# An earlier weight load, row-tiled products and a square root by Newton steps in a convolution network on one core

## The chip, the core and the metric

The kernel runs on one core of a Trainium2 chip. Its time is the device time of one execution in microseconds (us), the median over several executions of the same program. The engines are TensorE (PE, with PEld for its weight loads), VectorE (DVE), ScalarE (ACT), GpSimd (POOL) and SyncE (SP), which issues most DMAs. Every engine takes its own instructions strictly in the order in which the program was written; they meet through semaphores.

## The reference

The input x has shape 4 x 32 x 32 x 16 (batch, height, width, channels). Four layers each add to it a function of its group norm:

```python
x = x + conv(gn(x), M0, W0, G0)
x = x + conv(gn(x), M1, W1, G1)
x = x + interval(gn(x), W0, b0, W1, b1, W2, b2)
x = x + conv(gn(x), M3, W3, G3)
```

`gn` takes 8 groups of 2 channels: for each batch and group it subtracts the mean over the image and both channels, and divides by the root of the variance plus 1e-5. `conv` is the costly part:

```python
kern = transpose(G, (0, 1, 5, 4, 2, 3)).reshape(h * w * f, c, 3, 3)
shifted = conv_general_dilated(x, kern, 'SAME')   # 1024 x 16 output planes of 1024
diff = relu(x - shifted)                          # for each i, j and each y, x
return einsum('ijyx,byxc->bijc', M, x) - einsum('ijyx,bijyxc->bijc', W, diff)
```

For each of 1024 positions ij and 16 filters there is a 3x3 convolution of the whole image, a relu, and a sum weighted by W. The product with M is called the first terms below.

`interval` takes the 32 x 32 image as a table over intervals (i, j). It forms running maxima and minima over all subintervals (`interval_pooling`), and then two steps of the form `g = sigmoid(f[i,k] @ Wf + r[k,j] @ Wr + b)`, `max over k`, and a last sigmoid of a product.

## The kernel before

**Tiling.** The two batches 2g and 2g+1 are one group g, with 2 x 16 = 32 channels (`GC`). There are three convolutions (layers 0, 1, 2 in the code) and two groups, hence 6 phases in the order (g0, layer 0), (g1, layer 0), (g0, layer 1) and so on; the interval layer lies between layers 1 and 2. A phase has 8 chunks of 128 output positions ij, which are the 128 rows of PSUM. A chunk has 32 steps, one for each filter f and batch b. There are 1536 steps. A unit is 4 filters, so 8 steps, and there are 192 units; the first two ("plain") are prepared in another way.

**A step.** It uses one pair of PSUM banks, `pc` (two banks of 128x512, since the image has 1024 points). Numbers are split into a high and a low part[...]; `ia`, `ib`, `iyz` and `im9` are arrangements of the shifted image, and `WU`, `WL`, `WD`, `W9` are the split weights of a unit (the first three are the tile `parts`). Each product has 64 rows; two of them, on the upper and lower halves of the array (row tiles 0 and 1), run side by side. `first_part` issues 8 products (L627) from `parts` with `ib` and `ia`, and ACT multiplies the pair by 1 + EPS (L663). `second_part` of the step before then adds 6 products with `iyz` and `im9`, and one DVE instruction (L680, output `junk`) takes min(sum, 0) times the W chunk `WT` and accumulates it to one column. The pool has four bank pairs, which rotate.

**Units.** The generator `prep_parts` prepares a unit's weights during the eight steps of another unit, one `yield` a step. Slot 1: DVE splits the high part off (L203). Slot 2: ACT writes W9 (L175). Slot 3: ACT writes WD (L236), POOL writes WL (L237) and adds to W9 (L238). Slot 4: ACT WU (L240), POOL four more (L241, L243, L245). Slot 5: `prep(u + 1)`, POOL's subtraction of the identity from the next unit's raw weights (L214). Slot 7: SP issues two DMAs that copy `parts` across partitions (L251), then `load_raw(u + RAWS)` (L110), 768 KB from HBM into one of two `raw` buffers; L203 of that unit waits for its L214. A unit is ready one to two units before its first use.

**Work beside the steps.** `behind(phase)` is a generator that prepares the next phase: norms, interval layer, the image's new arrangement, first terms. What it yields is the number of steps to go on before its next piece, or IDLE, or CALM; with these two it waits for a slot of the unit which says so. So it is interleaved at fixed places into every engine's order:

```python
may = next(parts, (IDLE, CALM)) if n or at >= FIRST else (IDLE, CALM)
...
wait -= 1
if wait <= 0 and (kind > 0 or kind in may):
    kind = wait = next(behind, 1 << 20)
```

`group_norm` sums on DVE (L316 to L337), forms the mean, `xc` and its square on POOL (L344 to L348), sums the squares, and takes the root of the variance on ACT (L358) and its inverse on DVE (L360), after which POOL writes the normalized image (L361) to `xn` or, for the interval layer, to `xi`. The root and the interval layer's sigmoid need different tables of ACT; a small activation of `spare` (L353) ahead of the root brings the table load before the value is there. After it, `before_conv` transposes (L375, DVE), writes to DRAM and back (`xs<-xt` L381, `raw<-xs` L392, SP), splits (`upper_x` L203, L280, L284), and places the parts (L298, L300 on SP, `iyz` L288 on POOL, L175 and L178). `interval_layer` transposes `xi` (L508, DVE), scans, and takes products: the right side in three pieces of 11 columns k (`right_side` L561, copied by ACT L564) and the left side (L548), then sums (POOL, L580), maxima (DVE, L587) and a sigmoid (L594), whose table is loaded by another activation of `spare` (L591).

Of the kernel before, what the change touches and what calls it, by code (L numbers as in the profile page):

```python
# [8 lines left out]
F32 = mybir.dt.float32  # L9
F32R = mybir.dt.float32r  # L10
I32 = mybir.dt.int32
AF = mybir.ActivationFunctionType
# [3 lines left out]
P = 128  # L16
# [28 lines left out]
def net_kernel(ctx: ExitStack, tc: tile.TileContext, x, xq, xi, convs, iv_w, iv_b, out):  # L45
# [174 lines left out]
    def prep_parts():  # L220

        for u in range(PLAIN, n_chunks * NU):
            parts = wpool.tile([P, 2, 3, FU, P], F32R, tag="parts", bufs=AHEAD + 1, name=f"parts_{u}")
            W9 = wpool.tile([P, FU, P], F32R, tag="W9", bufs=AHEAD + 1, name=f"W9_{u}")
            units[u] = [parts[:, :, k] for k in range(3)] + [W9]
            src = raws.pop(u)
            w8 = src[:, 0].rearrange("p f k -> p (f k)")  # L230
            WU, WL, WD = (parts[:, 0, k].rearrange("p f k -> p (f k)") for k in range(3))
            high = upper(src[:, 0:1], 1, f"w{u}")[:, 0]
            yield (IDLE,)
            halve(W9, src[:, 1], low_w)
            yield ()
            nc.scalar.activation(WD, high, AF.Copy, scale=-EPS)  # L236
            nc.gpsimd.tensor_tensor(WL, w8, high, ALU.subtract)  # L237
            nc.gpsimd.tensor_tensor(W9, W9.bitcast(F32), src[:, 2], ALU.add)  # L238
            yield ()
            nc.scalar.copy(WU, high)  # L240
            nc.gpsimd.tensor_tensor(WD, WD.bitcast(F32), WL.bitcast(F32), ALU.add)  # L241
            for lo, hi in QUARTERS:
                nc.gpsimd.tensor_copy(WU[hi], WL[lo].bitcast(F32))  # L243
            for lo, hi in QUARTERS:
                nc.gpsimd.tensor_copy(WL[lo], high[hi])  # L245
            yield ()
            prep(u + 1)
            yield (IDLE,)
            yield (IDLE, CALM)
            for h in range(2):  # L250
                nc.sync.dma_start(  # L251
                    parts[64 * h : 64 * h + 64, 1].bitcast(F32),
                    parts[64 - 64 * h : 128 - 64 * h, 0].bitcast(F32),
                )
            load_raw(u + RAWS)
            yield (IDLE, CALM)
            yield (IDLE, CALM)

# [50 lines left out]
    def pair_view(ap):  # L309
        return ap.rearrange("p t (g s) -> p t g s", s=2)  # L310

    def group_norm(g, name, dst, gap):


        def sums(src):
            nc.vector.tensor_reduce(  # L316
                part[:, : GC // 2], src.rearrange("p t (g s) -> p g t s", s=2), axis=AX.XY, op=ALU.add
            )

        def totals(name):  # L320
# [26 lines left out]
        sq = work.tile([P, NT, GC], F32, tag="sq", name=f"sq_{name}")  # L347
        nc.gpsimd.tensor_tensor(sq, xc, xc, ALU.mult)  # L348
        yield 4
        sums(sq)  # L350
        yield gap
        yield IDLE
        nc.scalar.activation(spare, spare, AF.Sqrt)  # L353
        v = yield from totals(f"v{name}")
        yield 2
        yield IDLE
        rstd = work.tile([P, GC // 2], F32, tag="rstd", name=f"rstd_{name}")
        nc.scalar.activation(rstd, v, AF.Sqrt, bias=eps, scale=1.0 / (2 * NP))  # L358
        yield 2
        nc.vector.reciprocal(rstd, rstd)  # L360
        nc.gpsimd.tensor_tensor(pair_view(dst), pair_view(xc), spread(rstd), ALU.mult)  # L361
        yield 3

# [54 lines left out]
    def first_terms(layer, mt):  # L418


        sums = bank_pair(f"pf_{layer}")
        for g in range(NG):
            for pt in range(NT):
                for j in range(4):
                    nc.tensor.matmul(  # L425
                        sums[32 * j : 32 * j + 32, g, :256],
                        lhsT=xns[g][:, pt, :], rhs=mt[:, pt, j, :],
                        start=pt == 0, stop=pt == NT - 1, tile_position=(0, 32 * j),
                    )
        ft = work.tile([P, NG, NT * GC], F32, tag="fs", name=f"ft_{layer}")  # L430
        for g in range(NG):
            nc.vector.transpose(ft[:, g], sums[:, g, : NT * GC])
        yield 1
        for g in range(NG):
            nc.vector.tensor_tensor(
                X[g], X[g], ft[:, g].rearrange("p (t m) -> p t m", t=NT), ALU.add
            )
            yield 1
# [7 lines left out]
    def constants():  # L446
        nc.sync.dma_start(wv, iv_w)
        nc.sync.dma_start(bv, iv_b)
        mask2 = const.tile([P, GB], F32, name="mask2")
        nc.vector.tensor_reduce(  # L450
            mask2, ident.rearrange("p (s b c) -> p b s c", b=GB, c=C), axis=AX.XY, op=ALU.add
        )

        nc.gpsimd.tensor_scalar_mul(mask2[GC : 2 * GC], mask2[GC : 2 * GC], -1.0)
        yield 2

        def blocks(dst, k, mask, n, p0=0):
            p = dst.shape[0]
            nc.gpsimd.tensor_tensor(
                dst,  # L460
                wv[p0 : p0 + p, k, :].unsqueeze(1).to_broadcast([p, n, C]),
                mask[p0 : p0 + p].unsqueeze(2).to_broadcast([p, n, C]),
                ALU.mult,
            )

        nc.gpsimd.memset(rt, 0.0)
        yield 1


        for k, hidden, name in ((0, None, "f0"), (3, 2, "f1"), (6, 5, "f2")):  # L470
            n = 64 if hidden is None else 96
            t = const.tile([n, GB, C], F32, name=name)
            blocks(t[:64], k, mask2, GB)
            if hidden is not None:
                blocks(t[64:], hidden, mask2, GB, 64)
            iv[name] = t.rearrange("p k c -> p (k c)")
            yield 1
        for k, name in ((1, "r0"), (4, "r1")):
            t = const.tile([64, NQ * GB, C], F32, name=name)
            for q in range(NQ):  # L480
                blocks(t[:, q * GB : (q + 1) * GB, :], k, mask2, GB)
            iv[name] = t.rearrange("p k c -> p (k c)")
            yield 1
    def interval_layer(g):
# [37 lines left out]
        def running(dst, src):  # L522
# [16 lines left out]
            out=r[:R, :H, 1:], in_=table(one), pattern=[[-1, H], [1, H]], compare_op=ALU.is_ge,  # L539
            fill=0.0, base=0, channel_multiplier=0,  # L540
        )
        yield 5

        def left(name, wf):
# [9 lines left out]

        def right_side(name, wr):

            for k0 in range(0, T1, 11):
                j0 = k0 + 1
                ps = bank(f"ps_{name}{g}{k0}")
                n = T1 - j0  # L560
                nc.tensor.matmul(  # L561
                    ps[:, : 11 * n], lhsT=wr, rhs=r[:R, k0 : k0 + 11, j0:], start=True, stop=True
                )
                nc.scalar.copy(  # L564
                    rt[:, j0:, k0 : k0 + 11],
                    ps[:, : 11 * n].rearrange("p (k j) -> p j k", j=n),
                )
                yield 1

        def step(name, ftp, bias):  # L570
# [17 lines left out]
                last = t  # L588
                yield 6 if i < QI else 3
            yield IDLE  # L590
            nc.scalar.activation(spare, spare, AF.Sigmoid)  # L591
            yield 2
            yield IDLE
            nc.scalar.activation(s, s, AF.Sigmoid, bias=bias)  # L594
# [385 lines left out]
```

## Time and profile before

| quantity | value |
|---|---|
| median of 3 runs | 2479.14 us |
| lowest and highest | 2478.43 and 2481.91 us |
| the profiled execution, its time | 2478.41 us |
| span of its trace | 2476.7 us |
| granted TensorE clock | 1.0 of full speed |
| busy: PE / PEld / DVE / ACT / POOL | 99 / 84 / 84 / 76 / 64 % of the span |
| L680 `junk`, 1536 times | 1224 ns each |
| L663, 1520 times | 1008 ns each |
| L627, 21504 matmuls in four groups | 379 to 388 ns each, two at a time |
| POOL of a unit: L237, L238, L241 / L243, L245 / L214 | 1308, 1303, 1299 / 608, 609 / 1052 ns |
| one raw load, issue to landing | 7.1 us |
| DMA, share of 16 engines | some 53 % |

A row of the profile names an operation by its line, engine and tile. The busy shares are averages over the span; what a change at one place is worth is read from the timeline around that place.

### The profile page before, as it was taken

To read this page: it belongs to the slowest core of one execution; us is meant where nothing else is said; L and a number is where in the kernel's file an instruction comes from. 1 tells how busy PE (TensorE), PEld (TensorE's weight loads), DVE (VectorE), ACT (ScalarE), POOL (GpSimd) and SP (SyncE) were. 2 spreads that over 40 slices of the span, in tenths; PEclk is the share of its full clock that TensorE was granted. 3 is DMA by queue.
4 is the path that set the end of the run, shared out by engine and by line. 5 is a ranking of instruction groups with operands and counts; after the bars stand their busy time and mean duration, and the time that the engine had idled before them with its cause. 6 is when DMAs were issued, how large, how long until landed. Compare 5 with 4: busy or idle time off the path is not lost.

```text
span 2476.7 us, 58058 instructions
## 1 busy us (share of the span) xinstructions
PE 2458.2 (99%) x21906; PEld 2090.1 (84%) x21906; DVE 2087.3 (84%) x3617; ACT 1878.4 (76%) x2181; POOL 1579.7 (64%) x1750
## 2 busy tenths in 40 slices
PE   8999999999999999999999999999999999999999
PEld 5999888888888888888888988888998888888887
DVE  9888878888888888778898988899889888788887
ACT  4778767787777778777777777787777787677776
POOL 4766655666565657555567777586878676555552
PEclk9999999999999999999999999999999999999999
DMA  6446754466454467644454545574455467554442
GB/s 198 138 137 182 203 155 135 124 182 164 133 143 135 135 168 198 186 116 134 136 145 127 142 124 140 146 196 125 126 138 144 127 181 195 154 148 137 137 137 54
DMA packets 97673, 366.92 MB, mean 148 GB/s; under 512 B 26480, under 2 KB 31472, under 8 KB 97392
## 3 DMA queue, kind: packets, MB, share of 16 engines
q1 hardware_dynamic: 96832, 362.79, 53.0%
q8 instruction: 172, 2.82, 0.5%
q14 instruction: 109, 0.89, 0.1%
q10 hardware_dynamic: 432, 0.39, 0.1%
q0 software_dynamic: 128, 0.02, 0.0%
HBM read 199.78 MB, written 1.02 MB: 81 GB/s over the span
## 4 chain that ended last, share of the span: by engine, by line
PE 94%; DVE 2%; issue 1%; DMA 1%; ACT 0%; SPq 0%; POOL 0%; ACTq 0%; DVEq 0%; POOLq 0%
PE pc L627 93%; DVE junk L680 1%; PE pf L425 1%; DMA raw<-in_g 1%; ACT pc L663 0%; DMA first<-in_g 0%; SPq L298 0%; DVE raw L846 0%; SPq L300 0%; PE ps_l L548 0%; PE ps_r L561 0%; DMA parts<-parts 0%; DVE tables L508 0%; DVE raw L854 0%; DMA ib<-first 0%
## 5 line engine op out<-in xcount | busy, mean ns | idle before, releaser
L680 DVE SCALAR_TENSOR_TENSOR junk<-pc,WT 128x1024 f32<-128x1024 f32 x1536 | 1879.5, 1224 | 359.1 <-PE pc L627 308.3
L663 ACT ACTIVATE pc<-pc 128x1024 f32<-128x1024 f32 x1520 | 1532.0, 1008 | 561.0 <-PE pc L627 535.8
L627 PE MATMUL pc<-ib,parts 64*128 64x512 f32 x6080 | 958.5, 388 | 4.1 <-DVE junk L680 3.4
L627 PE MATMUL pc<-iyz,parts 64*128 64x512 f32 x6080 | 955.5, 387 | 2.2 <-ACT pc L663 2.0
L627 PE MATMUL pc<-ia,parts 64*128 64x496 f32 x6080 | 933.5, 379 | 0.0
L627 PEld LDWEIGHTS pc<-ia,parts 64*128 64x128 f32 x6080 | 595.5, 184 | 100.8
L627 PEld LDWEIGHTS pc<-ib,parts 64*128 64x128 f32 x6080 | 591.5, 184 | 105.0 <-DVE junk L680 9.9
L627 PEld LDWEIGHTS pc<-iyz,parts 64*128 64x128 f32 x6080 | 592.5, 184 | 88.4 <-ACT pc L663 6.4
L627 PE MATMUL pc<-im,W 64*128 64x496 f32 x3072 | 611.5, 384 | 0.0
L237 POOL TENSOR_TENSOR parts<-raw,upper_w 128x512 fp32r<-128x512 f32 x190 | 248.5, 1308 | 500.2 <-DVE upper_w L203 434.8
L627 PEld LDWEIGHTS pc<-im,W 64*128 64x128 f32 x3072 | 303.0, 184 | 54.5 <-issue 3.2
L243 POOL CAST parts<-parts 32x512 fp32r<-32x512 f32 x380 | 231.1, 608 | 50.1 <-ACT parts L240 31.8
L238 POOL TENSOR_TENSOR W<-W,raw 128x512 fp32r<-128x512 f32 x190 | 247.6, 1303 | 1.8 <-ACT W L175 1.8
L241 POOL TENSOR_TENSOR parts<-parts 128x512 fp32r<-128x512 f32 x190 | 246.8, 1299 | 2.0 <-ACT parts L236 1.9
L245 POOL CAST parts<-upper_w 32x512 fp32r<-32x512 f32 x380 | 231.6, 609 | 22.8
L214 POOL TENSOR_TENSOR raw<-raw,ident 128x512 f32<-128x512 f32 x190 | 199.9, 1052 | 52.2 <-DMA raw<-in_g 28.7
L175 ACT ACTIVATE W<-raw,low_w 128x512 fp32r<-128x512 f32 x190 | 136.2, 717 | 0.1
L680 DVE DVE_READ_ACCUMULATOR junk<-pc,WT 128x1 f32 x1536 | 127.5, 83 | 0.0
L236 ACT ACTIVATE parts<-upper_w 128x512 fp32r<-128x512 f32 x190 | 118.8, 625 | 6.6 <-DVE upper_w L203 6.4
L240 ACT CAST parts<-upper_w 128x512 fp32r<-128x512 f32 x190 | 116.5, 613 | 0.0
L695 POOL TENSOR_SCALAR acc<-acc 128x32 f32<-128x32 f32 x40 | 16.4, 409 | 141.7 <-DVE junk L680 139.7
L203 DVE TENSOR_SCALAR upper_w<-raw 128x512 int32<-128x512 int32 x190 | 86.1, 453 | 1.2 <-POOL raw L214 0.9
(139 smaller groups left out, 479.4 us busy)
## 6 DMA issues: line engine op xcount, KB each, us to landing
raw<-in_g SPq DMA_DIRECT2D x190, 768.0 KB, 7.1
parts<-parts SPq DMA_DIRECT2D x380, 384.0 KB, 4.9
WT<-in_w SPq DMA_DIRECT2D x48, 512.0 KB, 4.6
MT<-in_mt SPq DMA_DIRECT2D x24, 512.0 KB, 7.4
raw<-xs SPq DMA_DIRECT2D x120, 71.8 KB, 2.9
ib<-temp SPq DMA_DIRECT2D x40, 128.0 KB, 2.6
ia<-temp SPq DMA_DIRECT2D x80, 62.0 KB, 3.4
ib<-first SPq DMA_DIRECT2D x8, 128.0 KB, 2.4
```

Source lines behind the costliest of these rows:

```text
L175: nc.scalar.activation(dst, src, AF.Copy, scale=mask[:, 1:2])
L214: eng.tensor_tensor(raws[u][:, s, at:to], raws[u][:, s, at:to], pick[s][:, f0 + at : f0 + to].unsqueeze(2).to_broadcast([P, to - at, P]), ...
L236: nc.scalar.activation(WD, high, AF.Copy, scale=-EPS)
L237: nc.gpsimd.tensor_tensor(WL, w8, high, ALU.subtract)
L238: nc.gpsimd.tensor_tensor(W9, W9.bitcast(F32), src[:, 2], ALU.add)
L240: nc.scalar.copy(WU, high)
L241: nc.gpsimd.tensor_tensor(WD, WD.bitcast(F32), WL.bitcast(F32), ALU.add)
L243: nc.gpsimd.tensor_copy(WU[hi], WL[lo].bitcast(F32))
L245: nc.gpsimd.tensor_copy(WL[lo], high[hi])
L627: nc.tensor.matmul(ps[:, h, at : at + n], lhsT=w[r], rhs=v[r] if n == NH else v[r][:, :n], start=first and k == 0, stop=k == len(pairs) - ...
L663: nc.scalar.activation(ps, ps, AF.Copy, scale=1.0 + EPS)
L680: nc.vector.scalar_tensor_tensor(junk, ps.rearrange("p h n -> p (h n)"), 0.0, chunks[n], op0=ALU.min, op1=ALU.mult, accum_out=accs[phase][ ...
```

## The change

Five edits.

1. In `prep_parts` the subtraction `prep(u + 1)` is written two slots earlier (behind L238 in slot 3, ahead of L241), and `load_raw(u + RAWS)` three slots earlier (at the end of slot 4).
2. `right_side` uses one bank pair. The piece of 352 columns runs on row tile 0 into bank 0, the pieces of 231 and 110 on row tile 1 into bank 1. For that the lower 64 partitions need a copy of r, `below` (POOL), and the constants r0 and r1 are made on 128 partitions.
3. `group_norm` takes the inverse root without ACT: POOL forms a = v / (2 NP) + 1e-5, DVE forms a first value y from a's bits with a shift and a subtraction, and POOL improves it in four rounds y = y (1.5 - 0.5 a y y) of four instructions each, with the pauses 1, 1, IDLE, 2 ahead of them.
4. With it go the root's activation of `spare` and, in the interval layer, the sigmoid's.
5. The sigmoid's activation of `spare` is issued once, behind the products of layer 0's first terms.

```diff
             nc.gpsimd.tensor_tensor(W9, W9.bitcast(F32), src[:, 2], ALU.add)
+            prep(u + 1)
             yield ()
             nc.scalar.copy(WU, high)
...
                 nc.gpsimd.tensor_copy(WL[lo], high[hi])
+            load_raw(u + RAWS)
             yield ()
-            prep(u + 1)
             yield (IDLE,)
             yield (IDLE, CALM)
             for h in range(2):
...
-            load_raw(u + RAWS)
             yield (IDLE, CALM)
             yield (IDLE, CALM)
...
+    def inverse_root(v, name):
+
+        n = GC // 2
+        a, y, t = (
+            work.tile([P, n], F32, tag=tag, name=f"{tag}_{name}") for tag in ("root_a", "root_y", "root_t")
+        )
+        nc.gpsimd.tensor_scalar(a, v, 1.0 / (2 * NP), 1e-5, op0=ALU.mult, op1=ALU.add)
+        nc.vector.tensor_scalar(
+            t.bitcast(I32), a.bitcast(I32), 1, None, op0=ALU.logical_shift_right
+        )
+        nc.vector.tensor_scalar(
+            y.bitcast(I32), t.bitcast(I32), -1.0, float(0x5F3759DF), op0=ALU.mult, op1=ALU.add
+        )
+        nc.gpsimd.tensor_scalar_mul(a, a, -0.5)
+        for pause in (1, 1, IDLE, 2):
+            yield pause
+            nc.gpsimd.tensor_tensor(t, a, y, ALU.mult)
+            nc.gpsimd.tensor_tensor(t, t, y, ALU.mult)
+            nc.gpsimd.tensor_scalar(t, t, 1.5, None, op0=ALU.add)
+            nc.gpsimd.tensor_tensor(y, y, t, ALU.mult)
+        return y
...
-        nc.scalar.activation(spare, spare, AF.Sqrt)
         v = yield from totals(f"v{name}")
-        yield 2
-        yield IDLE
-        rstd = work.tile([P, GC // 2], F32, tag="rstd", name=f"rstd_{name}")
-        nc.scalar.activation(rstd, v, AF.Sqrt, bias=eps, scale=1.0 / (2 * NP))
-        yield 2
-        nc.vector.reciprocal(rstd, rstd)
+        rstd = yield from inverse_root(v, name)
         nc.gpsimd.tensor_tensor(pair_view(dst), pair_view(xc), spread(rstd), ALU.mult)
...
+        if layer == 0:
+            nc.scalar.activation(spare, spare, AF.Sigmoid)
         ft = work.tile([P, NG, NT * GC], F32, tag="fs", name=f"ft_{layer}")
...
-        nc.gpsimd.tensor_scalar_mul(mask2[GC : 2 * GC], mask2[GC : 2 * GC], -1.0)
+        for at in (GC, 3 * GC):
+            nc.gpsimd.tensor_scalar_mul(mask2[at : at + GC], mask2[at : at + GC], -1.0)
...
-            t = const.tile([64, NQ * GB, C], F32, name=name)
+            t = const.tile([P, NQ * GB, C], F32, name=name)
...
+        below = tables[R:, : T1 * T1].rearrange("p (i j) -> p i j", j=T1)
+        nc.gpsimd.tensor_copy(below, r[:R])
+        tops = (r[:R], below)
         yield 5
...
-            for k0 in range(0, T1, 11):
+            ps = bank_pair(f"ps_{name}{g}")
+            blocks = []
+            for k0, h, at in ((0, 0, 0), (11, 1, 0), (22, 1, 11 * (T1 - 12))):
                 j0 = k0 + 1
-                ps = bank(f"ps_{name}{g}{k0}")
                 n = T1 - j0
+                blocks.append((k0, j0, n, ps[:, h, at : at + 11 * n]))
                 nc.tensor.matmul(
-                    ps[:, : 11 * n], lhsT=wr, rhs=r[:R, k0 : k0 + 11, j0:], start=True, stop=True
+                    blocks[-1][3], lhsT=wr[R * h : R * h + R], rhs=tops[h][:, k0 : k0 + 11, j0:],
+                    start=True, stop=True,
                 )
+            for k0, j0, n, sums in blocks:
                 nc.scalar.copy(
...
             yield IDLE
-            nc.scalar.activation(spare, spare, AF.Sigmoid)
             yield 2
```

More of the change, by code (lines that the diff above doesn't have):

```diff
@@ L555, in right_side @@
         def right_side(name, wr):
-            for k0 in range(0, T1, 11):
+            ps = bank_pair(f"ps_{name}{g}")
+            blocks = []
+            for k0, h, at in ((0, 0, 0), (11, 1, 0), (22, 1, 11 * (T1 - 12))):
                 j0 = k0 + 1
-                ps = bank(f"ps_{name}{g}{k0}")
                 n = T1 - j0
+                blocks.append((k0, j0, n, ps[:, h, at : at + 11 * n]))
                 nc.tensor.matmul(
-                    ps[:, : 11 * n], lhsT=wr, rhs=r[:R, k0 : k0 + 11, j0:], start=True, stop=True
+                    blocks[-1][3], lhsT=wr[R * h : R * h + R], rhs=tops[h][:, k0 : k0 + 11, j0:],
+                    start=True, stop=True,
                 )
+            for k0, j0, n, sums in blocks:
                 nc.scalar.copy(
-                    rt[:, j0:, k0 : k0 + 11],
-                    ps[:, : 11 * n].rearrange("p (k j) -> p j k", j=n),
+                    rt[:, j0:, k0 : k0 + 11], sums.rearrange("p (k j) -> p j k", j=n)
                 )
```

## The prediction

> **What bounds the kernel.** I read the page first (busy shares, the chain that ended last), then the waits, then timelines around the places where TensorE stops.
>
> ```profile
> PE 2458.2 (99%) x21906; PEld 2090.1 (84%) x21906; DVE 2087.3 (84%) x3617; ACT 1878.4 (76%) x2181; POOL 1579.7 (64%) x1750
> PE 94%; DVE 2%; issue 1%; DMA 1%; ACT 0%; SPq 0%; POOL 0%; ACTq 0%; DVEq 0%; POOLq 0%
> L237 POOL TENSOR_TENSOR parts<-raw,upper_w 128x512 fp32r<-128x512 f32 x190 | 248.5, 1308 | 500.2 <-DVE upper_w L203 434.8
> ```
>
> TensorE is the bound and idles 18.5 us of 2476.7, 12 of it before the first 50 us; POOL mostly waits. So the change can win only at the few stops left, and it can make new ones. In the PE timelines one step (14 products) starts every 1.57 us. Four bank pairs rotate, so the reduction L680 (`junk`) of step j must end before the first product of step j+4, which without a stop starts 3.81 us after the second part of j (1284.72 to 1288.53). One stop shows the rule, in the DVE and PE timelines:
>
> ```profile
> 1283.67 1.31 DVE L508 STREAM_TRANSPOSE tables<-xi 32x256 f32<-32x256 f32 x2
> 1286.28 1.30 DVE L508 STREAM_TRANSPOSE tables<-xi 32x256 f32<-32x256 f32 x2
> 1287.61 1.23 DVE L680 SCALAR_TENSOR_TENSOR junk<-pc,WT 128x1024 f32<-128x1024 f32 x1
> 1288.90 0.73 PE L627 MATMUL pc<-ib,parts 64*128 64x512 f32 x4 [0.21 <-DVE junk L680]
> ```
>
> The junk ends at 1288.84 with its accumulator, TensorE starts at 1288.90 instead of 1288.53: 0.37 lost, and about 0.11 more to refill (the next product pair is 0.33 apart instead of 0.22). DVE may thus be about 1.5 us late unpunished.
>
> **What the Trainium skill says.** "ScalarE: Activation LUTs", What ACT_TABLE_LOAD costs: 1283 ns per load, plus a drain; the ACT timeline agrees on 1283 ns. "Perfetto Trace Analysis", Tensor Engine Instruction: ACT, DVE and GpSimd run strictly in order, and ends of matmuls are estimates; so a late POOL result blocks the DVE instruction and every junk behind it. "DMA: Bandwidth & Descriptors", Queues, rings and completion order: on each DMA engine the descriptors of one queue are taken in ring order; the trace agrees: small loads issued behind `raw<-in_g` (1594.84) landed at 1604.1 to 1605.1, just after its 1603.94. "TensorEngine Tiling (Array Packing)", Gotcha 1: different row tiles write to different banks; the change puts its two halves in two banks.
>
> **Part 1, table loads.** The program's order on ACT has five loads before and two after: the one at the start, and one behind layer 0's first terms, where TensorE has 7.04 us of other products (L425), so it costs nothing. Four go, each a stop like this one:
>
> ```profile
> 1564.04 1.28 ACT L353 ACT_TABLE_LOAD   x1
> 1565.33 0.20 ACT L353 ACTIVATE spare<-spare 1x1 f32<-1x1 f32 x1
> 1565.44 1.00 ACT L663 ACTIVATE pc<-pc 128x1024 f32<-128x1024 f32 x1
> ```
>
> TensorE's product at 1566.49 came 0.55 late, the other three (1422.63, 1834.35, 1978.16) 0.54 to 0.55; with refill 4 x 0.66 = **-2.6**. What is late next there is DVE, by the root below.
>
> **Part 2, right products.** Now three PSUM pairs are taken in three steps and the matmuls (0.59, 0.40, 0.20 us, twelve instructions seen as 24 passes) use one row tile. From the first product at 1326.41 to 1334.77 four steps took 8.36; less 4 x 1.57 and L548's 0.58 leaves 1.49 for L561; the other three calls give 1.37 to 1.51. After, 352 columns on one tile run beside 231+110 on the other: at best 0.59, with imperfect overlap 0.9. I take 0.7 saved per call (bounds 0.5 and 0.85): **-2.8**. `below` costs POOL one copy per interval layer (64x1089; by L534's 2.2 or L243's 1.2 ns per element, 1.3 to 2.4 us), hidden by the yield of five steps; the larger constants by POOL's idle time.
>
> **Part 3, roots.** Slots of `behind` do not move: the pauses 1, 1, IDLE, 2 equal the old 2, IDLE, 2. ACT loses 8 x 0.48, DVE a reciprocal of 0.25, and gains two small operations (L799, also 128 partitions by few columns, takes 0.23). POOL gains 18 per norm: 0.25 each (L344, 128x16, 252 ns; L696, 128x32, 254), 0.085 between dependent ones (L695 to L696): 1.3 per round, 5.1 for four. DVE now waits for POOL's `a` at once: 0.06 + 0.25 + 0.07 if POOL is free, up to 0.8 in layers 0 and 1, where the unit ends later by the moved L214. That is below 1.5 us: free, but for some 0.2 at each of the two layer-2 norms, where DVE is already late: **+0.4**. In layers 0 and 1 the rounds fit before the same `xn`, since POOL sits idle there 7.6 or waits for the acc.
>
> Not so in the interval and layer-2 norms. POOL's order puts `a` ahead of a whole unit that today starts before it:
>
> ```profile
> 1269.62 1.30 POOL L237 TENSOR_TENSOR parts<-raw,upper_w 128x512 fp32r<-128x512 f32 x1 [5.45 <-DVE upper_w L203]
> 1270.88 1.29 POOL L238 TENSOR_TENSOR W<-W,raw 128x512 fp32r<-128x512 f32 x1
> 1276.18 1.04 POOL L214 TENSOR_TENSOR raw<-raw,ident 128x512 f32<-128x512 f32 x1
> 1279.30 0.68 POOL L361 TENSOR_TENSOR xi<-xc_i,rstd_i 128x256 f32<-128x256 f32 x1 [2.08 <-DVE rstd_i L360]
> ```
>
> After: `a` waits for L337, which ends at 1272.11, so 1272.2; `a`, DVE's two and -0.5 to 1273.0; L237, L238, L214 to 1276.6; round one to 1277.9; L241, L243, L245 (1.3 + 2.7) to 1281.8; three rounds to 1285.6; `xi` to 1286.3. L508 stands in DVE's order at 1283.67: 2.65 late. L508 x2 then end at 1287.68, junk with accumulator 1289.02 against 1286.96: 2.1 + 0.11; the next pair and junk end 1291.7 against 1290.7: 1.0 + 0.1. 3.3 against today's 0.48: +2.8, twice: **+5.6**. The layer-2 norms likewise: L337 ends 1569.71, `xn` ends 1583.9 against 1577.6 today; L375 in its place at 1581.31 waits 2.6, and its junk ends 1585.7 against 1584.60: 1.2 each, **+2.4**.
>
> **Part 4, moves.** The subtraction L214 now stands before L241: a unit's parts are 1.05 later, with 8.9 us median between landing and use (from pairing each landing of `parts` with its first product). The raw load three steps sooner waits for POOL's L238 on SP, ahead of WT, xs and place transfers, and its 768 KB (7.1 us) come ahead of the parts' own. In steady state that is covered by the same 8.9. At the start it helps: the load leaves SP at about 25.3 instead of 35.39 and no longer holds the last `ib` until 50.38: TensorE's 0.8 + 0.1 stop at 50.52 goes: **-0.9**. At 1607.21 upper_x waited for xs transfers held by that load: 0.68 + 0.11, **-0.8**. Unit 42 (1.1 us of cover) and 125 (1.8): +0.2 each, **+0.4**. The tightest unit is 124, on SP:
>
> ```profile
> 1581.78 5.26 SPq L381 DMA_DIRECT2D xs<-xt  x8
> 1587.82 5.70 SPq L392 DMA_DIRECT2D raw<-xs  x12
> 1593.68 1.11 SPq L251 DMA_DIRECT2D parts<-parts  x2
> 1594.84 1.36 SPq L110 DMA_DIRECT2D raw<-in_g  x1
> SPq L392 <- DMA raw<-in_g: 20.9, 8, 3.0
> ```
>
> Its parts land 5.3 after the second issue, 1599.5; its first product is at 1600.27. The load moves from behind them to between `xs<-xt` and `raw<-xs`. `xs<-xt` starts 2.6 later (L375) and ends 1588.3 to 1589.7; the load lands 7 later, and the eighth DMA behind it reuses its semaphore and waits for that (the last line shows such waits): 1595 to 1597; five more and the parts go at 1597.5 to 1599.6 and land 1603.2 to 1605.3, against 1600.27 + 1.2: 1.7 to 3.8, I take 2.8. Unit 156 by the same steps: use at 2011.88 + 1.2, landing 2014.8 to 2015.5: 2.1. **+4.9**.
>
> **Sum.** -2.6 -2.8 -0.9 -0.8 = -7.1; +0.4 +5.6 +2.4 +0.4 +4.9 = +13.7; net +6.6. The profiled run took 2478.41 (span 2476.7 and 1.7 around it), the median 0.7 more: 2479.14 + 6.6 = **2485.7**.
>
> **Rivals.** *Late parts stay hidden*: only DVE's stops come; -7.1 + 8.8 = +1.7, 2480.8, no change. For it: cover is read from modelled ends, and xs issues are uneven (5.26 here, 3.8 at 1993). Against: the load stands first in SP's order. *Faster*: POOL absorbs the rounds. If an operation of 16 columns takes 0.16 with its gap instead of 0.32, `xi` and `xn` come under 0.3 late instead of 2.6; nothing is lost at L508 and L375, parts leave 2.3 earlier, and -7.1 + 1.5 = -5.6, 2473.5. The point where it decides is 2.5 us for four rounds; against it are both rows of 250 ns. *More*: if right products gain only 0.5 and the late parts reach the upper end at both units: +9.5, and a few us more where DVE's backlog meets L178 (1.9 us beside POOL): 2489 to 2492. *It does not do what it says*: a load might return with another function; the order shows none.
>
> **Chances.** The forecast with its upper end 0.58, hidden parts 0.25, faster 0.17. About 0.2% (5.0 us) is what a measurement of this kernel can tell from no change. Range 2473 to 2491: from the faster rival's time to near the upper end.
>
> **What would show it.** Right: ACT loads 5 to 2; DVE idle before L508's and L375's successors with POOL `xi`, `xn` as releaser, 2 to 3 us each; PE stops of 2 to 3 us at units 124 and 156 with the DMA of parts as releaser; no stop near 50 us. Wrong: `xi` ending before L508's turn, Newton rows under 0.2 us, or the span below 2475.

## The result and the profile after

The changed kernel takes 2486.88 us (median of 7 runs, 2485.95 to 2489.18) against 2479.14 before (7 runs, 2477.67 to 2481.91): a ratio of 1.0032, 95% interval 1.0022 to 1.0042, so 7.7 us slower. The profiled execution took 2486.47, its span is 2484.8, 8.1 more than before. Line numbers are those of the changed kernel here: L627 has become L651, L663 L687, L680 L704, L337 L359, L361 L377, L375 L391, L392 L408, L508 L527, L251 L252; Newton's instructions are L318 (a), L319 and L322 (first value), L325, and L328 to L331 (a round).

The page of the changed kernel, its busy shares and the chain that ended last:

```profile
PE 2459.8 (99%) x21906; PEld 2082.7 (84%) x21906; DVE 2086.4 (84%) x3625; ACT 1871.4 (75%) x2159; POOL 1604.9 (65%) x1897
...
PE 92%; DVE 3%; issue 1%; POOL 1%; DMA 1%; SPq 0%; ACT 0%; DVEq 0%; POOLq 0%; ACTq 0%
```

TensorE has as many instructions as before, yet it stands 25.0 us instead of 18.5 (span less busy) and is busy for 1.6 longer, and POOL has entered the chain with 1%. ACT is less busy by 7. So nothing became a new steady bound; the time went into single stops, and these are read in timelines.

First the interval norm near 1285, in POOL's timeline (start, duration, engine, line, operation, tiles):

```profile
1272.59 0.20 POOL L318 TENSOR_SCALAR root_a_i<-whole_vi 128x16 f32<-128x16 f32 x1 [8.25 <-DVE whole_vi L359]
...
1275.82 1.04 POOL L214 TENSOR_TENSOR raw<-raw,ident 128x512 f32<-128x512 f32 x1
1276.82 0.21 POOL L328 TENSOR_TENSOR root_t_i<-root_a_i,root_y_i 128x16 f32<-128x16 f32 x1
...
1280.63 1.36 POOL L246 CAST parts<-upper_w 32x512 fp32r<-32x512 f32 x2
1282.08 0.22 POOL L328 TENSOR_TENSOR root_t_i<-root_a_i,root_y_i 128x16 f32<-128x16 f32 x1
...
1285.52 0.22 POOL L331 TENSOR_TENSOR root_y_i<-root_y_i,root_t_i 128x16 f32<-128x16 f32 x1
1285.82 0.68 POOL L377 TENSOR_TENSOR xi<-xc_i,root_y_i 128x256 f32<-128x256 f32 x1
```

One round stands between the subtraction and the unit's casts, three behind them; `xi` ends at 1286.50. Each round takes 1.25 (1282.08 to 1283.33): its four instructions are 0.22 to 0.25 long, and some 0.08 lies between each and the next, which reads its result. What waits for `xi` is in DVE's timeline:

```profile
1282.84 1.23 DVE L704 SCALAR_TENSOR_TENSOR junk<-pc,WT 128x1024 f32<-128x1024 f32 x1 [0.17 <-PE pc L651]
1283.98 0.08 DVE L704 DVE_READ_ACCUMULATOR junk<-pc,WT 128x1 f32 x1
1286.53 1.26 DVE L527 STREAM_TRANSPOSE tables<-xi 32x256 f32<-32x256 f32 x2 [2.46 <-POOL xi L377]
1287.82 1.22 DVE L704 SCALAR_TENSOR_TENSOR junk<-pc,WT 128x1024 f32<-128x1024 f32 x1
```

and behind that junk TensorE, in its own timeline:

```profile
1289.11 0.74 PE L651 MATMUL pc<-ib,parts 64*128 64x512 f32 x4 [1.67 <-DVE junk L704]
...
1291.69 0.73 PE L651 MATMUL pc<-ib,parts 64*128 64x512 f32 x4 [0.70 <-DVE junk L704]
```

DVE stands 2.46 in front of a transpose that had not waited before, and TensorE starts one step 1.83 late and the next another 1.01; with the refill behind them it loses 3.0 here, against 0.5 at the same place before.

The second place is unit 124. SP's timeline (issues), and TensorE's:

```profile
1584.39 4.36 SPq L397 DMA_DIRECT2D xs<-xt  x8
1588.85 0.39 SPq L110 DMA_DIRECT2D raw<-in_g  x1
1590.34 7.21 SPq L408 DMA_DIRECT2D raw<-xs  x12
1597.72 1.11 SPq L252 DMA_DIRECT2D parts<-parts  x2
```

```profile
1603.67 0.49 PE L651 MATMUL pc<-ib,parts 64*128 64x512 f32 x1 [1.38 <-DMA parts<-parts]
```

The transfers of xs begin 2.6 later than before, the raw load stands between them, and the unit's parts, issued from 1597.72 instead of 1593.68, land at 1601.74 and 1603.63. The unit's first products start at 1601.37. The fourth, which needs the second landing, could have run at about 1601.6 and is 2.1 late; its row shows 1.38 because the products ahead of it count as busy until 1602.28.

The third is unit 157, 15 us behind the stop at unit 156 and not in the prediction. Its parts were issued at 2020.28 and landed at 2031.37, behind a raw load issued at 2019.75. TensorE's timeline, and a table of windows (the window and its length; busy time and number of instructions of PE, PEld, DVE, ACT and POOL; granted TensorE clock, DMA share, GB/s):

```profile
2031.41 0.49 PE L651 MATMUL pc<-ib,parts 64*128 64x512 f32 x1 [1.21 <-DMA parts<-parts]
```

```profile
2020.00:2029.00 9.00, 9.00 (x83) 8.99 (x81) 7.84 (x13) 8.31 (x12) 7.31 (x8) 1.00 0.96 238
2029.00:2032.00 3.00, 1.65 (x13) 0.84 (x11) 1.32 (x4) 1.33 (x2) 2.74 (x5) 1.00 0.74 270
2032.00:2034.00 2.00, 2.00 (x16) 1.62 (x14) 0.75 (x1) 1.01 (x1) 2.00 (x3) 0.70 0.95 211
2034.00:2036.00 2.00, 2.00 (x13) 1.60 (x12) 1.29 (x3) 1.12 (x2) 1.58 (x2) 0.50 0.85 233
```

Behind the stop the trace has a granted clock of 0.50 from 2032.78 to 2036.19, 3.41 us long: pairs of products start 0.41 apart in place of 0.22, which costs another 1.6 on top of the 2.1 of the stop.

### The profile page after: what moved, and what is told of

Its sections match the earlier page's. It is cut to its first block, busy times and chain, and to the rows that moved or that the text cites. A ratio compares the mean times of both kernels' runs of the same rounds, so it can differ in the third digit from the quotient of the medians.

```text
span 2484.8 us, 58159 instructions
## 1 busy us (share of the span) xinstructions
PE 2459.8 (99%) x21906; PEld 2082.7 (84%) x21906; DVE 2086.4 (84%) x3625; ACT 1871.4 (75%) x2159; POOL 1604.9 (65%) x1897
## 4 chain that ended last, share of the span: by engine, by line
PE 92%; DVE 3%; issue 1%; POOL 1%; DMA 1%; SPq 0%; ACT 0%; DVEq 0%; POOLq 0%; ACTq 0%
PE pc L651 91%; DVE junk L704 2%; PE pf L441 1%; DMA parts<-parts 1%; ACT pc L687 0%; SPq L408 0%; DMA raw<-in_g 0%; DVE raw L870 0%; SPq L397 0%; POOL parts L237 0%; POOL parts L242 0%; PE ps_l L570 0%; DVE upper_w L203 0%; POOL parts L246 0%; POOL W L238 0%
## 5 line engine op out<-in xcount | busy, mean ns | idle before, releaser
L704 DVE SCALAR_TENSOR_TENSOR junk<-pc,WT 128x1024 f32<-128x1024 f32 x1536 | 1879.0, 1223 | 357.3 <-PE pc L651 300.0
L687 ACT ACTIVATE pc<-pc 128x1024 f32<-128x1024 f32 x1520 | 1532.3, 1008 | 577.8 <-PE pc L651 551.8
L651 PE MATMUL pc<-ib,parts 64*128 64x512 f32 x6080 | 957.2, 388 | 11.8 <-DVE junk L704 7.4
L651 PE MATMUL pc<-iyz,parts 64*128 64x512 f32 x6080 | 951.4, 387 | 1.2 <-ACT pc L687 1.1
L651 PE MATMUL pc<-ia,parts 64*128 64x496 f32 x6080 | 930.4, 379 | 0.0
L651 PEld LDWEIGHTS pc<-ib,parts 64*128 64x128 f32 x6080 | 588.6, 184 | 117.8 <-DVE junk L704 15.7
L651 PEld LDWEIGHTS pc<-ia,parts 64*128 64x128 f32 x6080 | 591.0, 184 | 103.6
L651 PEld LDWEIGHTS pc<-iyz,parts 64*128 64x128 f32 x6080 | 588.5, 184 | 87.1 <-ACT pc L687 4.1
L651 PE MATMUL pc<-im,W 64*128 64x496 f32 x3072 | 607.3, 384 | 0.0
L237 POOL TENSOR_TENSOR parts<-raw,upper_w 128x512 fp32r<-128x512 f32 x190 | 248.1, 1306 | 520.0 <-PE pc L651 471.2
L651 PEld LDWEIGHTS pc<-im,W 64*128 64x128 f32 x3072 | 300.5, 184 | 55.8 <-issue 3.4
L246 POOL CAST parts<-upper_w 32x512 fp32r<-32x512 f32 x380 | 233.5, 614 | 22.8
L238 POOL TENSOR_TENSOR W<-W,raw 128x512 fp32r<-128x512 f32 x190 | 247.3, 1301 | 1.1 <-ACT W L175 1.1
L242 POOL TENSOR_TENSOR parts<-parts 128x512 fp32r<-128x512 f32 x190 | 246.0, 1295 | 0.3 <-ACT parts L236 0.2
L704 DVE DVE_READ_ACCUMULATOR junk<-pc,WT 128x1 f32 x1536 | 127.1, 83 | 0.0
L236 ACT ACTIVATE parts<-upper_w 128x512 fp32r<-128x512 f32 x190 | 118.8, 625 | 5.2 <-DVE upper_w L203 5.2
L241 ACT CAST parts<-upper_w 128x512 fp32r<-128x512 f32 x190 | 116.6, 614 | 0.0
L203 DVE TENSOR_SCALAR upper_w<-raw 128x512 int32<-128x512 int32 x190 | 85.4, 450 | 0.6 <-POOL parts L246 0.4
```

Source lines behind the costliest of these rows:

```text
L651: nc.tensor.matmul(ps[:, h, at : at + n], lhsT=w[r], rhs=v[r] if n == NH else v[r][:, :n], start=first and k == 0, stop=k == len(pairs) - ...
L687: nc.scalar.activation(ps, ps, AF.Copy, scale=1.0 + EPS)
L704: nc.vector.scalar_tensor_tensor(junk, ps.rearrange("p h n -> p (h n)"), 0.0, chunks[n], op0=ALU.min, op1=ALU.mult, accum_out=accs[phase][ ...
```

## The experiments

All were timed beside the kernel before on the same chip; ratios are to that kernel, with 95% intervals. The ledger numbers come from pairing ACT's 1520 scale instructions (L663, now L687) of two traces: where their distance in time grows, the later kernel has lost. A trace is one execution; executions of one kernel spread by 3 us and more, so a trace says where, and the ratio how much.

**1. The moves undone.**

```diff
-            prep(u + 1)              # behind L238
...
-            load_raw(u + RAWS)       # behind the casts
...
+            prep(u + 1)              # behind the casts, one slot later
...
+            load_raw(u + RAWS)       # behind the parts' DMAs
```

> The changed kernel with the subtraction and the raw load back in their old places; roots, right products and table loads stay as changed. Theory (the raw load ahead of other transfers on SP makes the parts of units 76, 124, 156 and 157 late, some 6.4 us together, and a dip of TensorE's clock behind the last of them cost 1.6): these stops vanish, those that the late parts covered come back (the image's transfers at 1607, DVE's backlog near 1635 and 2033, some 2 us), DVE's two stops at each interval norm (about 3 us) and the one at each layer-2 norm (about 1.3 us) stay; 2480 to 2482.5 us, 1 to 3 us over before. Rival (the parts are late because POOL has 18 more instructions in each norm): the stops by late parts stay, over 2484 us.

1.0025 (1.0016 to 1.0035), so 6.0 us slower than before: twice what the theory allowed. The late parts of units 76, 156 and 157 and the low clock did go, but unit 124 still loses 1.8 by late parts, as the rival had it: the Newton rounds alone put the transfers of xs 2.7 later, and the parts stand behind them. And smaller stops that the changed kernel did not have come back with some 4 us in the ledger, where 2 were expected. The loss at the norms stays, but by another path, which had been overlooked: with the subtraction in its old place, two Newton rounds stand ahead of it in POOL's order, and the next unit's L203 waits for it. DVE's timeline of this kernel:

```profile
1282.71 0.43 DVE L203 TENSOR_SCALAR upper_w<-raw 128x512 int32<-128x512 int32 x1 [2.00 <-POOL raw L214]
...
1285.90 1.30 DVE L527 STREAM_TRANSPOSE tables<-xi 32x256 f32<-32x256 f32 x2 [0.26 <-POOL xi L377]
```

The wait of 2.46 before the transpose has become 2.00 + 0.26 at two places; the loss per interval norm, 2.3, is that of the changed kernel (2.5). So the earlier subtraction takes a wait off L203 in the norms, and that wait comes back at the transpose.

**2. Only the raw load undone.**

```diff
             prep(u + 1)              # stays behind L238
...
-            load_raw(u + RAWS)       # behind the casts
...
+            load_raw(u + RAWS)       # behind the parts' DMAs
```

> The changed kernel with only the raw load back in its old place; the subtraction stays two steps sooner. Theory (the load's place on SP alone makes parts late): no stop by late parts at units 76, 124, 156, 157; the subtraction costs only where it runs beside a long DVE instruction (units 42 and 167, 0.3 to 0.4 us each); 2480.5 to 2483 us. Rival (the subtraction ahead of the casts delays the parts by 1.05 us and the tight units with it): stops by late parts stay at 124 and 156, 1 us or more each, over 2483 us.

1.0902 (1.0887 to 1.0916): 223 us slower, far outside both theories. The two moves depend on each other. The load of a unit was issued about four steps (6.3 us) ahead of its subtraction, lands 7.1 us later, and what stands behind the subtraction in POOL's order now is the rest of the current unit. The waits of this kernel:

```profile
POOL raw L214 <- DMA raw<-in_g: 817.8, 175, 10.2
```

175 of 190 subtractions wait for their load, 4.7 us each, and the wait feeds itself. POOL's timeline and below it SP's:

```profile
100.76 1.04 POOL L214 TENSOR_TENSOR raw<-raw,ident 128x512 f32<-128x512 f32 x1 [5.81 <-DMA raw<-in_g]
104.41 1.27 POOL L246 CAST parts<-upper_w 32x512 fp32r<-32x512 f32 x2
```

```profile
105.71 1.38 SPq L251 DMA_DIRECT2D parts<-parts  x2
107.20 0.86 SPq L110 DMA_DIRECT2D raw<-in_g  x1
```

The casts stand behind the waiting subtraction, the parts' DMAs behind the casts, and on SP the next load behind these DMAs. Once round this loop takes 13.5 us (medians of this trace: 7.1 from a load's issue to its landing, 0.1 to the subtraction, 5.1 to the parts' DMAs, 1.2 to the next load), while a unit's eight steps take 12.5. One us too much on 190 units is most of the 223. A step that is brought forward must bring its own input forward by as much.

**3. The root undone.**

```diff
-        rstd = yield from inverse_root(v, name)
...
+        nc.scalar.activation(rstd, v, AF.Sqrt, bias=eps, scale=1.0 / (2 * NP))
...
+        nc.vector.reciprocal(rstd, rstd)
```

> The changed kernel with the old root: ACT's root and DVE's reciprocal, with the small activations ahead of root and sigmoid in their old places. Theory (Newton rounds make xi and xn late): the stops at the interval and layer-2 norms fall back to those of before (gain 4.9 + 2.5 + 0.6 for the short waits for the root's first value), the four table loads come back (loss 2.9): about 2482 us, late parts as in the changed kernel. Rival (the interval stop comes from the unit's subtraction, which now stands ahead of the casts): the stops of 3 us stay, 2487 us or more.

1.0003 (0.9995 to 1.0011): 7.2 us gained by undoing one part, and no stop of 3 us left; the first pair of transposes starts at 1283.69, as in the kernel before. The gain is larger than the 5.1 expected, since units 124, 156 and 157 lose less too (1.5, 0.8 and 0.8 in place of 2.2, 1.7 and 2.1), and no low clock follows. This is the largest single cause.

**4. Two Newton rounds.**

```diff
         for k, pause in enumerate((1, 1, IDLE, 2)):
             yield pause
+            if k not in (0, 1):
+                continue
```

> The changed kernel with two Newton rounds in place of four, at the first two of the four pauses; the pauses stay. Half of the rounds' work on POOL is left out, so the root is less exact. Theory (each round takes 1.27 us of POOL ahead of xi or xn): xi ends some 2.5 us sooner, at or before DVE's turn for the transpose, and the stops of 3 us at each interval norm shrink to 0.5 or less, those of 1.3 us at the layer-2 norms to nothing: 2479 to 2481 us. Rival (DVE waits because the root's first value on POOL stands ahead of the unit, and the rounds are hidden): less than 1.5 us gained, over 2485 us.

1.0002 (0.9994 to 1.0011), 7.4 us less than four rounds. `xi` is there at DVE's turn, in its timeline:

```profile
1284.09 1.31 DVE L529 STREAM_TRANSPOSE tables<-xi 32x256 f32<-32x256 f32 x2
```

There is no releaser, so no wait; the stop behind the pair falls to 0.44, near the 0.37 of before, and those of 1.07 at the layer-2 norms are gone. The late parts are not: unit 124 loses 2.8 by them and unit 156 1.7.

**5. Two rounds and the moves undone.** The edits of 1 and 4 together.

> The changed kernel with two Newton rounds (a less exact root) and with subtraction and raw load back in their old places. Theory (in the old order the two rounds stand ahead of the subtraction in POOL's order, and DVE's L203 waits for that, 2.00 us in the run with the moves undone): DVE is still some 1.9 us late at each interval norm, so a stop of about 2 stays there in place of 0.4, and at the layer-2 norms little; xi itself is no longer waited for; with -2.9 for the table loads and -2.2 for the right products the sum is within 1 us of before. Rival (the moves only cost time, at units 124 and 156): 3 to 5 us faster than before.

1.0033 (1.0021 to 1.0046). The wait of L203 for the subtraction came as expected (2.02), and 2.4 per interval norm with it, but the sum is 8.2 slower, not near zero: the same wait appears at the layer-2 norms (1.4 each), and at 1660 a raw load landed so late that L203 waited 3.51 for its subtraction, 2.5 lost. Halving the rounds is worth 7 us with the moves and nothing without them. Late subtractions cost as much as a late `xi`.

**6. Right products alone.** The kernel before with `right_side`, `below` and the constants changed.

> The kernel before with the right products alone changed (one bank pair, two row tiles, the copy below, wider constants); root, table loads, subtraction and raw load as before. Theory (each of four calls gains 0.5 to 0.6 us of TensorE's time, read from the traces of before and changed): about 2.1 us faster than before, and up to 0.5 more where a stop of DVE's just ahead of a call shrinks. Rival (the gain seen in the changed kernel came from the stops around it): under 1 us.

0.9996 (0.9988 to 1.0004): the interval takes in no change and 3 us gained. The trace has the gain at the four calls, 0.56, 0.60, 0.54 and 0.50. TensorE's timeline of this kernel shows the call in one piece, where before three pieces lay in three steps:

```profile
1326.97 0.76 PE L589 MATMUL ps_r<-tables,r 64*128 64x352 f32 x6
```

So 2.2 is shown in the trace, and is too little for the timing to resolve.

**7 and 8. The parts' DMAs on ACT's queue**, with four and with two rounds.

```diff
-                nc.sync.dma_start(
+                nc.scalar.dma_start(
                     parts[64 * h : 64 * h + 64, 1].bitcast(F32),
```

> The changed kernel with the DMAs of parts issued on ACT's queue in place of SP's. Theory (parts are late because they are issued and served behind the raw load and the image's transfers on SP's one queue): the stops at units 76, 124, 156 and 157 go or fall under 0.5 us, those at the norms stay: 4 to 7 us faster than the changed kernel, 2480 to 2483 us. Rival A (the DMA engines are the limit there, busy 0.96 in that stretch): parts land as late, less than 2 us gained. Rival B (ACT waits in order for POOL's last cast ahead of the issue): new stops by ACT at the norms, over 2488 us.

> The same with two Newton rounds (a less exact root) in place of four. Theory: no late parts and no stop at the norms above that of before; the gains remain, some 2.9 (table loads) and 2.2 (right products): 2473 to 2475.5 us, faster than before by 3 to 5. Rival A (DMA engines the limit): as with two rounds on SP's queue, no difference to before. Rival B (ACT waits for POOL): slower than before.

1.0815 (1.0800 to 1.0830) and 1.0762 (1.0748 to 1.0777): rival B, at a size that nobody expected. ACT's timeline, and below it POOL's and TensorE's, at one of its stops:

```profile
1359.68 1.01 ACT L687 ACTIVATE pc<-pc 128x1024 f32<-128x1024 f32 x1 [0.56 <-PE pc L651]
1365.71 1.12 ACTq L252 DMA_DIRECT2D parts<-parts  x2
1366.93 1.93 ACT L687 ACTIVATE pc<-pc 128x1024 f32<-128x1024 f32 x2 [6.25 <-POOL root_y_i L331]
```

```profile
1364.41 1.27 POOL L246 CAST parts<-upper_w 32x512 fp32r<-32x512 f32 x2
```

```profile
1367.99 1.22 PE L651 MATMUL pc<-iyz,parts 64*128 64x512 f32 x4 [5.22 <-ACT pc L687]
```

The issue waits for POOL's last cast, and ACT's next scale waits behind it. The page names another POOL line as releaser (the root's); the issue goes 0.03 behind the end of L246. SP can afford that wait, an engine in the steps' loop cannot. With four rounds TensorE waits for ACT 65 times, 130.8 us in all; the rest of the 200 was not taken apart. Whether the DMAs would land in time on another queue is not told by these runs.

**9 and 10. The image's transfers two steps later**, with two and with four rounds.

```diff
-        yield 2
+        yield 4 if layer == 2 else 2     # between xs<-xt and raw<-xs
```

> Subtraction and raw load in the new places, two Newton rounds (a less exact root), and in the last convolution the 24 transfers raw<-xs two steps later (yield 4 in place of 2 behind xs<-xt), so that 4 of them stand ahead of the parts of units 124 and 156 on SP in place of 12. Theory (these parts lie ready on POOL's side at about 1586.5 and are late because they are issued only behind the twelve): they go some 4 us sooner and the stops at units 124 and 156 (2.4 and 1.4 us with two rounds) vanish; 2474 to 2476 us, 2 to 4 faster than before. Rival (the raw load ahead, 768 KB, is what holds them): the stops keep over 1 us each, no gain over two rounds alone.

> The changed kernel (four rounds) with the same later transfers. Theory: the stops by late parts at units 124 and 156 (2.2 and 1.7 us) vanish, those at the norms (about 3 us each interval norm, 1.3 each layer-2 norm) stay; if the stop at 157 and the low clock behind it go too, 2 to 3 us more: 2480 to 2483 us. Rival (four rounds make the image's chain so late that the transfers collide again behind it): new stops at upper_x or at the parts, no gain.

Two rounds: 0.9998 (0.9990 to 1.0006). The stops at 124 and 156 are gone, but the gain of 2 to 4 us over before did not come: the transfers now stand ahead of unit 125. TensorE's timeline of the two-round kernel:

```profile
1611.00 0.50 PE L653 MATMUL pc<-ib,parts 64*128 64x512 f32 x1 [0.47 <-DMA parts<-parts]
```

Four rounds: 1.0034 (1.0021 to 1.0048), the rival. Units 124 and 156 are in time; unit 125 loses 1.7 by late parts, and unit 157 4.6, with the clock at 0.50 again from 2030.96 on. The windows of this kernel:

```profile
2029.00:2032.00 3.00, 1.20 (x5) 0.80 (x7) 0.47 (x2) 0.14 (x1) 2.93 (x4) 0.83 0.99 322
2032.00:2034.00 2.00, 2.00 (x14) 1.58 (x12) 0.00 (x0) 1.01 (x1) 1.82 (x4) 0.50 0.49 198
```

So the place of the 24 transfers decides which unit is late, not whether one is. With two rounds the chain begins, counted in steps, only 0.2 later than before (the transfers of xs at 1579.10, where this kernel is 2.9 ahead), and still unit 125 loses 1.0: with the moved raw load among them, neither of the two places tried has room for all.

**11. DVE's turns later**, four rounds.

```diff
-        yield 3                          # between xi or xn and its transpose
+        yield 5 if gap == 2 else 4 if gap == 1 else 3
...
-                yield 1                  # between the two pairs of transposes
+                yield 2
```

with the edit of 9.

> The changed kernel (four rounds, exact as there) with later transfers as before and DVE's turns later: in the interval norm two steps more between xi and its transposes, one step more between xn and its transpose in the last convolution, and two steps in place of one between the two pairs of transposes of xi. Theory (Newton rounds cost only because DVE's in-order turn comes before xi and xn): stops at the norms fall to 0.5 us or less without a change of POOL's work, the table loads' and right products' gains remain: 2473 to 2477 us, faster than before. Rival (POOL's added work itself is the cost, it delays the units): stops of over 1 us at the norms stay or come back at the parts, 2479 or more.

1.0003 (0.9995 to 1.0012): 7.2 us less than the changed kernel, with all of POOL's instructions. Experiment 10 has the same later transfers with the old turns and stands at 1.0034, so the difference comes of the turns alone. DVE's timeline of this kernel:

```profile
1287.41 1.30 DVE L527 STREAM_TRANSPOSE tables<-xi 32x256 f32<-32x256 f32 x2
...
1291.38 1.29 DVE L527 STREAM_TRANSPOSE tables<-xi 32x256 f32<-32x256 f32 x2
```

Neither pair waits. No stop at the norms is over 0.6, and an interval norm loses 1.0 in all, against 3.0 in the changed kernel; what is left over are late parts at units 125 and 157 (2.0 and 1.2). At the norms it is the turn in DVE's order that costs, not POOL's work. The gain expected over before did not come.

**12. Newton on DVE**, moves undone, three rounds of three instructions.

```diff
...
+            nc.vector.tensor_tensor(t, y, y, ALU.mult)
+            nc.vector.scalar_tensor_tensor(t, t, -0.5, a, op0=ALU.mult, op1=ALU.mult)
+            nc.vector.scalar_tensor_tensor(y, t, 1.5, y, op0=ALU.add, op1=ALU.mult)
```

> Subtraction and raw load in their old places, right products and table loads as changed, and the Newton steps on DVE in place of POOL: the first value in three instructions at once, then three rounds of three instructions at three of the four pauses, some 0.25 us each. Theory (the cost was POOL's in-order queue: the rounds stood ahead of the subtraction, xi and xn): DVE gains 12 short instructions per norm, at most 0.7 us in one step, under the 1.5 us it may be late; xi and xn come as early as before, so no stop at the norms grows by more than 0.4: -2.9 (tables) and -2.2 (right products) remain, 2473 to 2476 us, 2 to 4 faster than before. Rival (DVE, 84% busy, has no room: its backlog of some 2.5 us per norm reaches TensorE at each norm): new stops of 1 us at several of the eight norms, 2478 us or more.

1.0022 (1.0014 to 1.0030), the rival. `xi` ends at 1278.56, 8 us sooner than with POOL's rounds, but DVE's small instructions are not all small. DVE's timeline of this kernel:

```profile
1270.43 1.30 DVE L318 TENSOR_SCALAR root_a_i<-whole_vi 128x16 f32<-128x16 f32 x1
1271.77 0.17 DVE L319 TENSOR_SCALAR root_t_i<-root_a_i 128x16 int32<-128x16 int32 x1
```

L318 takes 1.30 from 1270.43, while POOL's L241 runs from 1270.41 for 1.30: it ends with it. The small instructions do not all wait so: L319 takes 0.17 while POOL's next instruction, a cast, runs. TensorE stops at 1273.64, 1275.70 and 1289.64, where before it stopped at 1288.90 alone.

## Why the prediction held, and where its steps did not

The prediction was 2485.7, slower with a chance of 0.58; measured 2486.88. Its terms against the ledger of the two traces (us, rounded):

| step | predicted | measured |
|---|---|---|
| four table loads | -2.6 | -2.9 |
| right products | -2.8 | -2.2 |
| start, stop at 50.5 | -0.9 | -0.2 |
| upper_x wait near 1607 | -0.8 | -0.8 |
| wait for the root's first value | +0.4 | +0.5 |
| interval norms, both | +5.6 | +4.9 |
| layer-2 norms, both | +2.4 | +2.4 |
| parts at units 124 and 156 | +4.9 | +3.9 |
| units 42 and 125 | +0.4 | +0.4 |
| not foreseen: unit 157 | | +2.1, clock +1.6 |
| not foreseen: units 76 and 167 | | +0.9 |
| not foreseen: DVE's other stops, smaller | | -2.6 |
| sum | +6.6 | +8.1 |

That the sum came so near is in part luck. The terms that were forecast come to 6.0 against 6.6; what nobody foresaw is 4.6 lost and 2.6 gained, and leaves 2.0. Two figures of the prediction that do not enter its sum are wrong: TensorE stands 8.3 us before the first 50 (busy 41.67 of them), not 12, and the terms of the rival *More* come to 8.7, not 9.5.

**The path of the loss is as forecast.** POOL takes `a`, then a unit, then rounds; `xi` was put at 1286.3 and ended at 1286.50; DVE was to wait at the transpose, and did, 2.46. The runs with the old root, with two rounds and with later turns each bring an interval norm's 3.0 down to 1.0 or less and run 7 us faster than the changed kernel, by three different edits; a part of each 7 us is the smaller loss at unit 157 and the low clock that does not follow. The table loads are two in the trace, and each of the four places gains 0.7.

**Late parts, right place, wrong owner.** Issue and landing at unit 124 came as worked out (issue 1597.5 to 1599.6 forecast, 1597.72 and 1598.23 measured; landing 1603.2 to 1605.3 forecast, 1603.63 measured). But the prediction booked 4.9 to the moves. With the moves undone unit 124 still loses 1.8; with the old root it loses 1.5; with both as changed 2.2. Either change alone is enough to break the cover of 0.8 us. (Parts are not ready one to two units ahead, as the description of the kernel has it: the prediction's median of 8.9 us is less than one unit of 12.5.) By the timed ratios, on top of the right products the moves alone cost 1.7 us (1.0003 against 0.9996), and in the changed kernel about as much (1.0032 against 1.0025). The roots cost 7.2 with the moves (1.0032 against 1.0003) and 7.2 without (1.0025 against 0.9996). Each of these differences is uncertain by some 3 us, so the roots' 7.2 is shown and the moves' 1.7 is not told from zero.

**The start.** The stop at 50.52 went, as forecast, and 0.8 was expected of it. It seems to have let ACT and DVE catch up. In the changed kernel's ACT timeline L236 waits for DVE, and the scale behind it is late; TensorE stops one step on:

```profile
51.12 0.63 ACT L236 ACTIVATE parts<-upper_w 128x512 fp32r<-128x512 f32 x1 [0.48 <-DVE upper_w L203]
```

```profile
52.72 0.73 PE L651 MATMUL pc<-iyz,parts 64*128 64x512 f32 x4 [0.63 <-ACT pc L687]
```

The step that failed is "the stop goes: -0.9": what is late next there was not asked.

**Unit 42** lost 0.36 where 0.2 was forecast, and for another reason: its parts landed in time (553.77, first product 554.41), but DVE's L178 took 1.89 in place of 0.74, beside POOL's L288 and L237. Unit 167 is alike. DVE's timeline of the changed kernel:

```profile
2172.54 1.37 DVE L453 TENSOR_TENSOR X<-X,ft 128x256 f32<-128x256 f32 x1
```

Before it took 0.49. In both kernels POOL's addition to `WD` (L241, now L242, 1.3 long) runs beside it, and it ends 0.28 to 0.29 after that one. Before, it began 0.21 ahead of the addition's end; now, with the moved subtraction in front of the addition, it begins 0.21 after its start. "SBUF — State Buffer" of the Trainium skill, 🔬 SBUF: two separate sides, says that DVE and GpSimd share a port pair which one holds for a whole instruction; these traces agree, and so does the 1.30 against about 0.2 for 16 columns in the last experiment. A moved POOL instruction has a price on DVE that its own row doesn't show.

**Unit 157 and the clock.** The prediction stopped at 156. "TensorE: Matmul & The Clock Gate", Part 1, tells of a monitor that halves the clock by activity in windows of 3413 ns. The clock records of the traces agree. In the changed kernel the clock rose at 12.09 and fell at 2032.78, 592 times 3.4133 later, for 3.41; in experiment 10 it rose at 13.69 and fell 591 times 3.4133 later, again for 3.41. So it is decided window by window on a fixed grid, and what counts is how much falls into one window. In the window ahead of the fall (2029.37 to 2032.78) 13 products started, in that of experiment 10 five, where an undisturbed window has about 30. The longer stop of 2.8 with two rounds at unit 124 brought no low clock: a border of its grid, 1599.37, cuts it in two, and 19 and 18 products started on the two sides. In all traces of this case the clock fell behind every full-clock window with fewer than 10 starts and behind none with more than 14. Between these both occur, so the exact limit is open. All seven runs of the changed kernel have a mean clock of 0.998 to 1.000.

**Right products**: 0.54 a call; 0.7 was taken between the bounds 0.5 and 0.85, the lower would have been the better choice.

No version here is shown to be faster than the kernel before. The right products alone come nearest (0.9996).

## What to carry to other kernels

A small instruction in the order of an idle engine is not free: ask what stands ahead of it there and whose turn waits for its result, since on engines that run in order the wait stops everything behind it. A transfer or subtraction brought forward takes its neighbours' cover along: check its own input (the raw load under the subtraction, 223 us) and every consumer on the queue that it passes. And where two parts of a change lean on the same thin cover, undo them one at a time and together before booking the loss to one.

## What the runs showed of the hardware that was not expected

A DMA issue on ACT's queue holds ACT: 0.03 us after POOL's cast the issue goes, and ACT's next instruction had stood 6.25. A 128x16 instruction of DVE took 1.30 us where a POOL `TENSOR_TENSOR` of 1.30 had begun just ahead of it, and 0.17 beside the cast that followed. And the granted clock of TensorE fell to 0.50 for 3.41 us although TensorE was busy 2.06 of the 3.41 us ahead: what decided was a window of a fixed grid with 13 product starts in place of some 30, so that the same stop can cost the clock or not by where it falls.
